# Earlier layernorm statistics, a later copy and a turned order of products in a pre-layernorm attention and feed-forward kernel

## The chip, the cores and the metric

The kernel runs on one core of a Trainium2 chip. The metric is the device time of one execution in microseconds (us). A core has five engines with a queue of instructions each, which run side by side and wait for each other by semaphores: TensorE (PE, matrix products and transposes; PEld is its loading of weights), VectorE (DVE), ScalarE (ACT), GpSimd (POOL) and SyncE (SP), which here only starts copies by DMA. PE writes to PSUM, a small memory of banks; all else lies in SBUF or in DRAM.

## The reference

Sixteen sequences of 256 positions with 256 channels, all in float32. Each goes through attention and then through a quantised linear layer, both behind a layernorm and both added to what came in:

```python
x = x + attention(layernorm(x), wq, wk, wv, wo)
x = x + ffn(layernorm(x), weight, bias)
```

The layernorm takes off the mean and divides by the root of the variance plus 1e-5, per position; it has no weights. Attention has 16 query heads and 4 key and value heads of 128 channels. A query sees the first 4 positions (the sink) and the last 32 up to itself (the window):

```python
mask = (k <= q) & ((k < 4) | (k >= q - 31))
scores = einsum(q, k) / sqrt(128);  attn = masked_softmax(scores);  out = (attn @ v) @ wo.T
```

The ffn scales each row of its input and of the weight to 127, rounds to int8, multiplies, scales back and adds the bias:

```python
x_q = round(x / (max|x| / 127));  y = (x_q @ w_q.T) * x_scale * w_scale + bias
```

## The kernel before

**Units and places.** The work is cut into 128 units: 16 sequences (n), times 4 groups of heads (g), times 2 halves of the queries (t). One loop (`for i in range(len(units) + 2)`) goes through them; its round i is called place i here, and place i modulo 8 "place 0 to 7 of a sequence". In every place the scores of one unit are computed (L556, into `pss`), DVE scales and masks them (L567) and takes the row maxima (L569), ACT does the exponentials (L594), and DVE takes the sums against a floor (L601), their reciprocals (L602) and the product (L613). DVE then transposes the weights by blocks of 32 (L578), and SP brings them through DRAM into the layout that the next product needs: the store `zd` (L580), and, from the next place on, the load `ad` (L584). Two places after its scores the unit's weights meet the values (L619, `po`); ACT copies the result (L631, `oT`). In the first three and the last units there is no way through DRAM: PE transposes (L561) and ACT copies (L564, `ad`).

**The other work** is hung on places by tables (`at(place, function, list)`). Each queue runs in the order in which the instructions are written; no scheduler changes it. In a place the order is: scores; work listed as `begin`; output products of older units (`shares`); exponentials; `combine` of the queries asked for in the place before; values and weights product (`po`); a chunk of keys or values if the place has one (even places); normalisation; the next queries; POOL's `combine` of the chunk; DVE's `combine` of a finished output (in place 3); and last the list `small`.

**Seven products instead of eight.** The products of queries, keys, values and output, cut into 2 x 2 blocks of 128, are done with seven block products, as in Strassen's method. Sums of blocks are prepared by POOL (L257 to L266: `xs` of the input, `wq_sums` and the like of the weights, `os` of the attention's output). The seven products lie in two PSUM banks: 1, 2, 6 and 7 in the first, 4, 5 and 3 in the second. `products` yields them in an order that is an argument: 1, 2, 6, 7, 4, 5, 3 unless another is given (the queries), or `SMALL_FIRST`, that is 4, 5, 3, 1, 2, 6, 7 (keys and values). `combine` makes the result of the seven with five additions (L304 to L308): the first two read the first bank, the last three the second. DVE does it for the queries (`qt`) and the output (`pc`), straight from PSUM; POOL does it for keys and values (`ktmp`, `vt`), from copies that ACT makes of the two banks (`both_banks`, L325: second bank first). Queries use the two banks of the pool `ps_q`; a chunk of keys or values takes its second bank from `ps_q` and its first from `ps_m`, which has two banks and is also used for `po`. The output's seven products are summed over the groups of heads in the pool `ps_y`, which has one pair of banks: the next sequence's first output products (place 4, L674) can start when `combine` has read the last ones.

**The first layernorm of sequence n** is spread over the places from 8n - 14 on: `load_x` (L94) at 8n - 16, statistics (`statistics`, L183 and L185 on DVE, L187 and L188 on POOL) at 8n - 14, that is place 2 of sequence n - 2, the two normalisations (L193) two and four places after the statistics, and then the transposition by blocks (L387, through DRAM with L392 and L401) and the channel sums (L263 to L266). For sequences 1 and 2 the places are given by hand.

**The second layernorm and the ffn of sequence n** are six steps (`ffn_steps`) in places 4, 5, 6 of sequence n + 1 and 0, 1, 2 of sequence n + 2: statistics, normalising (with the bias on POOL, L729), scale (L710, L711), quantising (L715 and L717 on DVE, L720 and L721 on POOL), a transposing copy by SP (L724, `hT`), and the linear layer (L735 on PE, L740 on DVE, L741 on POOL, and the store L742).

**The tail.** The last sequence's output ends in two halves, which go through `last_steps` one after the other: `stats`, `quantise`, `turn`, `linear` (L758 to L794). The first half's `stats` and `quantise` are written at the end of place 127, its `turn` at the end of place 128.

Of the kernel before, what the change touches and what calls it, by code (L numbers as in the profile page):

```python
# [34 lines left out]
def kernel(  # L35
# [12 lines left out]
    pe, dve, act, pool, sp = nc.tensor, nc.vector, nc.scalar, nc.gpsimd, nc.sync  # L48
# [42 lines left out]
    def load_x(n):  # L91
        if n < B:
            xts[n] = xp.tile([P, NT, DM], FP, tag="x", name=f"x_{n}")
            sp.dma_start(xts[n], x_v[n])  # L94
# [4 lines left out]
    wv_sb = const.tile([P, NC, G * D], FP, name="wv_sb")  # L99
# [147 lines left out]
    def region(p, i):  # L247
        return p[REGION[i][0]][:, REGION[i][1]]
# [16 lines left out]
        pool.tensor_sub(t[2], b22, b12)  # L265
        pool.tensor_sub(t[3], b21, t[1])  # L266

    def products(p, factors, order=(1, 2, 6, 7, 4, 5, 3)):

        a, sa, b, sb = factors  # L270
        pairs = {
            1: (a[0][0], b[0][0]), 2: (a[0][1], b[1][0]), 6: (sa[1], sb[1]), 7: (sa[2], sb[2]),
            4: (a[1][1], sb[3]), 5: (sa[0], sb[0]), 3: (sa[3], b[1][1]),
        }
        for i in order:
            yield region(p, i), *pairs[i]
# [4 lines left out]
    SMALL_FIRST = (4, 5, 3, 1, 2, 6, 7)  # L281
# [5 lines left out]
    def banks_of_chunk(name):  # L287
        p = [ps_m.tile([P, NBLK, P], FP, tag="m", name=f"{name}_0"), q_bank(0, f"{name}_1")]
        turn_of[0] ^= 1
        return p  # L290
# [48 lines left out]
    wv_sums = const.tile([P, 4, 2, D], FP, name="wv_sums")  # L339
# [6 lines left out]
    def factors(n, w, sums, pair):  # L346

        a = [[w[:, c, (2 * pair + e) * D : (2 * pair + e + 1) * D] for c in range(NC)] for e in range(2)]
        return (
            a, [sums[:, i, pair % 2] for i in range(4)],  # L350
            xn_blocks(n), [xn_sums[n][:, i] for i in range(4)],
        )

    def xn_blocks(n):
        return [[xnT[n][:, c, j * P : (j + 1) * P] for j in range(NT)] for c in range(NC)]

    def norm_steps(n):
        def stats():
            mvs[n] = statistics(xts[n], range(NT), f"a{n}")

        def norm(t):
            if t == 0:
                xns[n] = p1.tile([P, NT, DM], FP, tag="xn", name=f"xn_{n}")
            standardise(xns[n], xts[n], mvs[n], [t])

        return [stats, lambda: norm(0), lambda: norm(1)]

    def channels(n):

        xn_sums[n] = p2.tile([P, 4, P], FP, tag="xs4", name=f"xs4_{n}")  # L370
        b = xn_blocks(n)
        right_sums([xn_sums[n][:, i] for i in range(4)], *b[0], *b[1])

    def turned(n):
        xnT[n] = p2.tile([P, NC, T], FP, tag="xnT", name=f"xnT_{n}")
        pt = ps_m.tile([P, NC, T], FP, tag="m", name=f"xt_{n}")
        for c in range(NC):
            for j in range(NT):
                pe.transpose(pt[:, c, j * P : (j + 1) * P], xns[n][:, j, c * P : (c + 1) * P], ident)
        dve.tensor_copy(xnT[n], pt)  # L380
        channels(n)
# [56 lines left out]
    def values_buffer(n, pair):  # L438
        vw[n, pair] = vws[pair]

    def values_to(n, pair, v, tiles=range(NT)):


        w, fresh = vw[n, pair], n == 0
        b0, b1 = tiles[0] * NBLK, (tiles[-1] + 1) * NBLK
        sp.dma_start(w[1:NKP:NCH, b0:b1], v[b0:b1].rearrange("b k d -> k b d"))
        c1 = min(b1 + 1, SB)
        sp.dma_start(w[0:NKP:NCH, b0 + 1 : c1], v[b0 : c1 - 1].rearrange("b k d -> k b d"))
        if b0 == 0:
            rows = QB if fresh else SINK  # L450
            sp.dma_start(w[2 : NCH * (rows - 1) + 3 : NCH], v[0, 0:rows].unsqueeze(1).to_broadcast([rows, SB, 2 * D]))
            if fresh:
                sp.dma_start(w[0:NKP:NCH, 0], v[0])
# [45 lines left out]

    def values(n, pair):  # L500
        p = banks_of_chunk(f"pv_{n}_{pair}")
        for to, left, right in products(p, factors(n, wv_sb, wv_sums, pair), SMALL_FIRST):
            pe.matmul(to, right, left, start=True, stop=True)  # L503
        v = p2.tile([P, 3, 2, D], FP, tag="vt", name=f"vt_{n}_{pair}")

        def rest():
            vd = dram.tile([T, 2 * D], FP, tag="vd", name=f"vd_{n}_{pair}")
            sp.dma_start(vd.rearrange("(j p) d -> p j d", p=P), v[:, 0:2].rearrange("p j e d -> p j (e d)"))
            values_buffer(n, pair)
            return lambda: values_to(n, pair, vd.rearrange("(b k) d -> b k d", k=QB))  # L510

        return Products(p, f"v_{n}_{pair}", (v[:, 0:3:2, 0], v[:, 2, 1], v[:, 1, 0], v[:, 0:2, 1])), rest
# [233 lines left out]
    def last_steps(j):  # L746

        n, tag = B - 1, f"last_{j}"  # L750
        py = pys[n][j][:, 0:2].rearrange("p i d -> p (i d)")
        d = p1.tile([P, 2, 3, D], FP, tag="ktmp", name=f"d_{tag}")[:, 0, 0:2].rearrange("p i d -> p (i d)")
        x2 = p1.tile([P, 6, D], FP, tag="pc", name=f"x2_{tag}")[:, 0:2].rearrange("p i d -> p (i d)")
        y = p1.tile([P, NT, DM], FP, tag="xn", name=f"y_{tag}")[:, 0]
        mv = p2.tile([P, nc.vector.BN_AGGR_DIM], FP, tag="mv2", name=f"mv_{tag}")
        top, by, xs, least = (p2.tile([P, 1], FP, tag=k, name=f"{k}_{tag}") for k in ("top", "by", "xs1", "least"))
        hT = p2.tile([P, NC, P], BF, tag="hT1", name=f"hT_{tag}")

        def stats():
            st = p2.tile([P, nc.vector.BN_STATS_DIM], FP, tag="st2", name=f"st_{tag}")  # L760
            dve.bn_stats(st, py)
            dve.bn_aggr(mv, st)

            pool.tensor_scalar(least, mv[:, 1:2], LN_EPS, 1e-24, ALU.add, ALU.mult)
            pool.tensor_tensor(least, least, root, ALU.pow)
            pool.tensor_scalar(mv[:, 1:2], mv[:, 1:2], LN_EPS, None, ALU.add)
            pool.tensor_tensor(mv[:, 1:2], mv[:, 1:2], half[:, 0:1], ALU.pow)
            dve.tensor_scalar(d, py, mv[:, 0:1], None, ALU.subtract)
            dve.tensor_reduce(top, d, AX.X, ALU.max, apply_absolute_value=True)
            act.copy(x2, py)  # L770

        def quantise():
            dve.tensor_scalar(top, top, 1.0 / 127.0, least, ALU.mult, ALU.max)
            dve.reciprocal(by, top)
            pool.tensor_mul(xs, top, mv[:, 1:2])
            for c in range(NC):
                k = d[:, c * P : (c + 1) * P]
                dve.tensor_scalar(k, k, by, MAGIC, ALU.mult, ALU.add)
                dve.tensor_scalar(k, k, MAGIC + 127.0, MAGIC - 128.0, ALU.min, ALU.max)

        def turn():
            for c in range(NC):
                pt = (ps_s, ps_t)[c].tile([P, P], FP, tag="st"[c], name=f"ht_{tag}_{c}")
                pe.transpose(pt, d[:, c * P : (c + 1) * P], ident)
                dve.tensor_scalar(hT[:, c], pt, MAGIC, None, ALU.subtract)
            dve.tensor_add(x2, x2, bias_bc)

        def linear():
            pa = ps_m.tile([P, DM], FP, tag="m", name=f"pa_{tag}")
            for c in range(NC):  # L790
                pe.matmul(pa, hT[:, c], wqfT[:, c, :], start=(c == 0), stop=(c == NC - 1))
            dve.scalar_tensor_tensor(y, pa, xs, wsc_bc, ALU.mult, ALU.mult)
            dve.tensor_add(y, y, x2)
            sp.dma_start(out_v[n, :, j], y)  # L794

        return [stats, quantise, turn, linear]


# [20 lines left out]
    def at(slot, f, what=small):  # L819
        what.setdefault(slot, []).append(f)  # L820
# [14 lines left out]
            at(n * PER + slot, (n, h), asked)  # L835
    for n in range(1, B):
        first = n * PER - 14
        places = (0, 1, 1, 2) if n == 1 else (4, 5, 6, 7) if n == 2 else (first, first + 2, first + 4, first + 5)
        for k, slot in enumerate(places[:3]):
            at(slot, lambda n=n, k=k: norm_steps(n)[k]())  # L840
        if n == 1:
            at(places[3], lambda n=n: turned(n))
        else:
            def turn(n=n, slot=places[3]):
                for k, f in enumerate(turned_by_blocks(n)):
                    at(slot + 1 + k, f, begin)
                at(slot + 2, lambda: channels(n))

            at(places[3], turn)
            at(max(first - 2, 0), lambda n=n: load_x(n))  # L850
    for i, (n, g, t) in enumerate(units):
        if n == 0:
            at(i + 2 + lag(i), lambda u=(n, g, t): projected(*u), shares)
# [157 lines left out]
```

## Time and profile before

| what | value |
|---|---|
| time, median of 3 runs | 780.27 us (780.01 to 780.97) |
| time of the profiled execution | 780.31 us |
| its span, first to last instruction | 778.5 us |
| mean granted TensorE clock | 0.998 |
| busy: PE, DVE, POOL, ACT | 758.6, 624.7, 512.7, 399.4 us |
| copies by DMA | 97.45 MB, mean 125 GB/s |

A profiled row of the timeline gives the start in us from the span's start, the duration in us, the engine, the source line, the operation, what it writes and reads (buffer numbers left out), how many instructions are merged into the row, and in brackets the idle time before it with what ended it. A row of waits gives the engine and line that waited, the engine and line that it waited for, the total in us, how often, and the longest. Busy time is an average over stages; what counts for the end is which wait ends last at a place. Spans on POOL are rough.

### The profile page before, as it was taken

Reading aid. Unit: us, or ns where it says so; the run is one execution under the profiler, and the core shown is the slowest. Engines: PE = TensorE matmul, PEld = TensorE weight load, DVE = VectorE, ACT = ScalarE, POOL = GpSimd, SP = SyncE. Lnnn points to the kernel's source line nnn. Section 1 sums busy time; section 2 is a strip of 40 time slices with the busy share of each in tenths; the row PEclk is TensorE's granted clock in tenths of the full one; section 3 lists DMA queues with packets and bytes.
Section 4 is the critical chain, followed back from the end, with each engine's and each line's share of the span. In section 5 each row is a group of like instructions: output and inputs, shape, how many; then the busy total and the mean of one; then the engine's idle time right before and its main releaser. Section 6 shows DMA issues by size and latency. Waiting matters only on the chain.

```text
span 778.5 us, 18824 instructions
## 1 busy us (share of the span) xinstructions
PE 758.6 (97%) x6483; PEld 744.0 (96%) x6483; DVE 624.7 (80%) x1775; ACT 399.4 (51%) x1561; POOL 512.7 (66%) x812
## 2 busy tenths in 40 slices
PE   9999999999999999999999999999999999999995
PEld 7989999999999999999999999999999999999994
DVE  2578978888788887888889788888888879887765
ACT  3555545555455455554555455554554554555551
POOL 4666977676665856757676675866658577576622
PEclk9999999999999999999999999999999999999999
DMA  7625354343534435344254543435344353443311
GB/s 241 208 86 139 112 143 133 104 122 122 153 114 137 124 94 162 117 139 137 86 137 125 148 128 106 131 111 160 117 134 122 98 154 117 130 138 101 95 44 35
DMA packets 150679, 97.45 MB, mean 125 GB/s; under 512 B 44984, under 2 KB 148792, under 8 KB 150584
## 3 DMA queue, kind: packets, MB, share of 16 engines
q1 hardware_dynamic: 150584, 96.24, 42.1%
q8 instruction: 52, 0.85, 0.4%
q14 instruction: 43, 0.35, 0.2%
HBM read 54.39 MB, written 39.85 MB: 121 GB/s over the span
## 4 chain that ended last, share of the span: by engine, by line
PE 86%; DVE 11%; issue 2%; ACT 0%; POOL 0%; DVEq 0%; POOLq 0%; ACTq 0%
PE pq L523 21%; PE py L674 21%; PE po L619 13%; PE pss L556 11%; PE pk L493 6%; PE pv L503 6%; PE py L658 3%; DVE scores L613 2%; PE pq L534 2%; DVE y L740 1%; DVE sm L601 1%; PE pa L735 1%; DVE nmax L569 1%; DVE scores L567 1%; DVE qt L306 1%
## 5 line engine op out<-in xcount | busy, mean ns | idle before, releaser
L594 ACT ACTIVATE scores<-scores,nmax 128x68 f32<-128x68 f32 x512 | 173.5, 340 | 259.5 <-DVE nmax L569 257.0
L619 PE MATMUL po<-ad,vw 96*128 96x128 f32 x1024 | 135.4, 275 | 0.8 <-ACT ad L564 0.8
L556 PE MATMUL pss<-kt,qt 128*128 128x68 f32 x1024 | 130.2, 268 | 0.0
L619 PEld LDWEIGHTS po<-ad,vw 96*128 96x128 f32 x1024 | 125.5, 192 | 2.1 <-ACT ad L564 1.5
L556 PEld LDWEIGHTS pss<-kt,qt 128*128 128x128 f32 x1024 | 126.1, 192 | 0.7 <-issue 0.5
L567 DVE SCALAR_TENSOR_TENSOR scores<-pss,masks 128x272 f32<-128x272 f32 x128 | 56.2, 439 | 83.9 <-PE pss L556 82.6
L523 PE MATMUL pq<-xs,wq_sums 128*128 128x128 f32 x714 | 118.6, 275 | 0.0
L523 PEld LDWEIGHTS pq<-xs,wq_sums 128*128 128x128 f32 x714 | 98.8, 192 | 0.0
L594 ACT ACTIVATION_READ_ACCUMULATOR scores<-scores,nmax 128x1 f32 x512 | 95.7, 187 | 0.0
L674 PE MATMUL py<-wo_sums,os 128*128 128x128 f32 x672 | 87.0, 279 | 0.0
L631 ACT COPY oT<-po 128x512 f32<-128x512 f32 x129 | 75.4, 585 | 22.2 <-PE po L619 22.2
L304 POOL TENSOR_TENSOR ktmp<-b_k 128x256 f32<-128x256 f32 x30 | 25.6, 853 | 90.1 <-ACT b_k L325 90.1
L674 PEld LDWEIGHTS py<-wo_sums,os 128*128 128x128 f32 x672 | 79.5, 192 | 0.0
L578 DVE STREAM_TRANSPOSE z<-scores 128x384 f32<-128x384 f32 x120 | 69.4, 578 | 4.1
L523 PE MATMUL pq<-xnT,wq_sb 128*128 128x128 f32 x476 | 72.6, 275 | 0.0
L257 POOL TENSOR_TENSOR os<-oT 128x256 f32<-128x256 f32 x56 | 41.0, 732 | 45.9 <-ACT oT L631 45.9
L674 PE MATMUL py<-wo_sb,oT 128*128 128x128 f32 x448 | 62.2, 282 | 8.5 <-DVE pc L305 8.5
L613 DVE TENSOR_TENSOR scores<-scores,sm 128x272 f32<-128x272 f32 x120 | 61.5, 513 | 4.1
L674 PEld LDWEIGHTS py<-wo_sb,oT 128*128 128x128 f32 x448 | 54.5, 192 | 9.9 <-issue 9.9
L523 PEld LDWEIGHTS pq<-xnT,wq_sb 128*128 128x128 f32 x476 | 62.7, 192 | 0.0
L569 DVE TENSOR_REDUCE nmax<-scores 128x4 f32<-128x272 f32 x128 | 55.8, 436 | 4.4
L304 POOL TENSOR_TENSOR vt<-b_v 128x256 f32<-128x256 f32 x30 | 21.9, 730 | 51.3 <-ACT b_v L325 51.3
(186 smaller groups left out, 1729.0 us busy)
## 6 DMA issues: line engine op xcount, KB each, us to landing
zd<-z SPq DMA_DIRECT2D x120, 192.0 KB
ad<-zd SPq DMA_DIRECT2D x120, 192.0 KB
vd<-vt SPq DMA_DIRECT2D x30, 256.0 KB
vw<-vd SPq DMA_DIRECT2D x30, 256.0 KB
vw<-vd SPq DMA_DIRECT2D x30, 224.0 KB
x<-in_x_dram SPq DMA_DIRECT2D x15, 256.0 KB
out_dram<-y SPq DMA_DIRECT2D x15, 256.0 KB
zxd<-zx SPq DMA_DIRECT2D x56, 64.0 KB
```

The costliest lines, as they stand in the source:

```text
L304: eng.tensor_add(c11_u, like(p[0][:, 0:2], c11_u), two(p1, c11_u))
L493: pe.matmul(to, left, right, start=True, stop=True)
L523: pe.matmul(to, left, right, start=True, stop=True)
L556: pe.matmul(pss[:, k, :], qt[n, g][:, t, k].rearrange("p h i -> p (h i)"), kt[n, g][:, t * NBLK + k, :], start=True, stop=True,)
L567: dve.scalar_tensor_tensor(s[:, :, 0:NK], pss, SCALE, masks[:, t], ALU.mult, ALU.add)
L569: dve.tensor_reduce(nmax, s[:, :, 0:NK], AX.X, ALU.max, negate=True)
L578: dve.transpose(z, s.rearrange("p k (c i) -> p c k i", c=NCH))
L594: act.activation(s[:, k, 0:NK], s[:, k, 0:NK], AF.Exp, bias=nmax[:, k : k + 1], scale=1.0, accum_out=sm[:, k : k + 1],)
L613: dve.tensor_mul(s, s, sm.unsqueeze(2).to_broadcast([P, NBLK, NK]))
L619: pe.matmul(po[:, k], vw[n, g // 2][:, t * NBLK + k, g % 2 * D : (g % 2 + 1) * D], ad[:, :, k], start=True, stop=True,)
L631: act.copy(o[:, t, hs].rearrange("p h (k i) -> p k h i", i=QB), po[:, :, hs])
L674: pe.matmul(region(py, i), left[:, e], right[:, e], start=(g == 0 and e == 0 and i in (1, 4)), stop=(g == G - 1 and e == 1 and i in (7, 3)),)
```

## The change

Three edits.

1. The first layernorm's statistics of sequences 3 to 15 are done two places earlier, at 8n - 16 (place 0 of sequence n - 2); the load of x is issued two places earlier too, at 8n - 18 (place 6 of sequence n - 3). Normalisations and the rest stay.
2. In the tail, ACT's copy of the first half's output (`x2`) is written in `turn` instead of `stats`, and so stands in ACT's queue behind the copy of the last transposed weights (`ad`) and the two copies `oT`. For the second half it stays.
3. The first values of sequence 1 (pair 0, place 6 of sequence 0) take their seven products in the order 1, 2, 6, 7, 4, 5, 3 instead of 4, 5, 3, 1, 2, 6, 7.

```diff
-    def products(p, factors, order=(1, 2, 6, 7, 4, 5, 3)):
+    LARGE_FIRST = (1, 2, 6, 7, 4, 5, 3)
+
+    def products(p, factors, order=LARGE_FIRST):
...
     def values(n, pair):
         p = banks_of_chunk(f"pv_{n}_{pair}")
-        for to, left, right in products(p, factors(n, wv_sb, wv_sums, pair), SMALL_FIRST):
+
+        order = LARGE_FIRST if (n, pair) == (1, 0) else SMALL_FIRST
+        for to, left, right in products(p, factors(n, wv_sb, wv_sums, pair), order):
             pe.matmul(to, right, left, start=True, stop=True)
...
             dve.tensor_reduce(top, d, AX.X, ALU.max, apply_absolute_value=True)
-            act.copy(x2, py)
+            if j:
+                act.copy(x2, py)
...
         def turn():
+            if not j:
+                act.copy(x2, py)
             for c in range(NC):
...
         first = n * PER - 14
-        places = (0, 1, 1, 2) if n == 1 else (4, 5, 6, 7) if n == 2 else (first, first + 2, first + 4, first + 5)
+        places = (0, 1, 1, 2) if n == 1 else (4, 5, 6, 7) if n == 2 else (first - 2, first + 2, first + 4, first + 5)
...
-            at(max(first - 2, 0), lambda n=n: load_x(n))
+            at(max(first - 4, 0), lambda n=n: load_x(n))
```

## The prediction

> **What bounds the kernel now.** First the page's top, for who is busy; then what TensorE (PE) waited for; then the instructions in order of time at the place of the largest wait.
>
> ```profile
> span 778.5 us, 18824 instructions
> PE 758.6 (97%) x6483; PEld 744.0 (96%) x6483; DVE 624.7 (80%) x1775; ACT 399.4 (51%) x1561; POOL 512.7 (66%) x812
> ```
> PE is the bound: an edit away from PE pays only where PE waits today. Its waits (total, times, longest) are few:
>
> ```profile
> PE py L674 <- DVE pc L305: 8.5, 12, 0.7
> PE ht_last L784 <- DVE d_last L779: 3.1, 2, 2.9
> PE pv L503 <- DVE qt L305: 1.2, 1, 1.2
> PE po L619 <- ACT ad L564: 0.8, 1, 0.8
> ```
> The first row is one wait in each of sequences 2 to 13: the next sequence's first output products (place 4 of 8) stand behind VectorE's (DVE) reading of the old ones in `combine`, at the end of place 3. Below is why DVE is late there, in the sequence around 361 us, and beside it sequence 14, around 692 us, the only one with this `combine` in which place 2 carries no first-layernorm statistics (no sequence 16 exists).
>
> ```profile
> 360.94 0.72 POOL L188 TENSOR_TENSOR mv_a<-mv_a,half 128x2 f32<-128x2 f32 x1
> 361.63 1.27 POOL L741 TENSOR_TENSOR y<-y,x 128x512 f32<-128x512 f32 x1
> 363.10 0.73 POOL L257 TENSOR_TENSOR os<-oT 128x256 f32<-128x256 f32 x1 [0.20 <-ACT oT L631]
> ...
> 690.77 1.27 POOL L741 TENSOR_TENSOR y<-y,x 128x512 f32<-128x512 f32 x1
> ```
> ```profile
> 362.19 0.72 DVE L601 TENSOR_TENSOR sm<-sm,floor 128x4 f32<-128x4 f32 x1
> 363.16 0.96 DVE L613 TENSOR_TENSOR scores<-scores,sm 128x272 f32<-128x272 f32 x1
> 365.08 0.29 DVE L305 TENSOR_TENSOR pc<-py,pc 128x128 f32<-128x128 f32 x1
> ...
> 692.47 0.16 DVE L601 TENSOR_TENSOR sm<-sm,floor 128x4 f32<-128x4 f32 x1
> 692.88 0.44 DVE L613 TENSOR_TENSOR scores<-scores,sm 128x272 f32<-128x272 f32 x1
> 694.28 0.29 DVE L305 TENSOR_TENSOR pc<-py,pc 128x128 f32<-128x128 f32 x1
> ```
> ```profile
> 365.51 1.13 PE L674 MATMUL py<-wo_sb,oT 128*128 128x128 f32 x8 [0.71 <-DVE pc L305]
> ...
> 694.92 1.11 PE L674 MATMUL py<-wo_sb,oT 128*128 128x128 f32 x8
> ```
> L601 is stretched to 0.72 us and ends at 362.91, when GpSimd's (POOL) L741 ends (362.90); L613 then falls into L257 and takes 0.96. In sequence 14 POOL has no L187/L188 to do before L741, which ends at 692.04, before L601 starts; both run at 0.16 and 0.44, and PE does not wait. So the delay comes not from DVE's own load (its statistics end at 358.12 and it then idles 0.74 us for PE) but from POOL being 1.00 us late (L187 starts 360.63, L741 361.63).
>
> **The change, part by part.**
>
> *Statistics of sequences 3 to 15, from place 2 to place 0.* Moved each time: two bn_stats and two bn_aggr on DVE (357.19 to 358.12, 0.93), L187 and L188 on POOL (1.00), and one 256 KB load of x, issued in place 6 instead of place 0 (issue 0.42 to 1.20 on SyncE's (SP) queue).
>
> What goes: 12 waits. Sequence 14 shows the whole price: from place 4's scores to place 5's takes 694.08 to 700.44 = 6.36 us there, 363.80 to 371.24 = 7.44 in the sequence shown. 1.08 each, 12 x 1.08 = 12.96. It is more than the row's 0.71 because PE also drags behind DVE after the wait (the keys' first products at 368.04, 0.15 after L305 of the queries). What is late next: at 697.24 PE starts the keys 0.15 after DVE's 697.09, so it is just DVE-bound there even then; 6.36 includes that.
>
> What it costs in place 0:
> ```profile
> 347.88 0.44 DVE L567 SCALAR_TENSOR_TENSOR scores<-pss,masks 128x272 f32<-128x272 f32 x1 [1.34 <-PE pss L556]
> ...
> 357.52 0.73 POOL L304 TENSOR_TENSOR vt<-b_v 128x256 f32<-128x256 f32 x1 [1.16 <-ACT b_v L325]
> ```
> DVE idles 1.34 us before place 1's scores; 0.93 fits, 0.41 is left. L717 (0.88, two instructions) slides beside POOL's adds of the keys, where such a pair costs up to 0.3 (L304 took 0.99 beside L717 instead of 0.73): about 0.1 is left. If that is gone, scores of place 1 come late by tenths, and the next cover is 0.88 of DVE idle at 353.01, while PE's first reuse of a query bank (350.41) stands 0.97 after DVE freed it (349.44). Cost 0, bounds 0 and, if DVE ran over by a whole 0.3 with no cover, 12 x 0.3 = 3.6.
>
> POOL: L720 and L721 (quantise), the four L257 to L260 and the four channel sums run 1.00 later, 356.36 becoming 357.36, and the 1.16 of idle before place 2's adds takes it: these wait for ScalarE's (ACT) copy until 357.52 anyway. Behind L720/L721 queue: the transposing copy L724 on SP (352.53, to about 353.1), behind it the weights' copy `ad` of place 1 (354.13, used 361.34) and, through the data, PE's L735 at 358.22. L724 was issued as late as 5.01 us before L735 (164.47 against 169.48) without a wait; 353.1 is 5.1 before. The sums `os` end at 355.6, used about 359.5; the channel sums are used three places later. Cost 0.
>
> SP: in place 6 the load now stands between `vd` (337.79) and the copy `ad` (338.32), which goes to about 338.8 and shares the engines with 256 KB more. Its reader is PE's po at 342.81, 4.0 us later. The nearest row is place 4's: `ad` issued at 363.41 right behind a 256 KB store, read at 367.02, 3.6 us, no wait. `vd`'s reader in place 7 and the later zd stay in order. In place 0 the load is gone from in front of `ad` (348.52). Cost 0; bounds 0 and 13 x 0.5 = 6.5, if it landed 0.5 us past its reader. x is read two places after its issue, as before.
>
> *Order of products in the second sequence's first values.* Place 6 of sequence 0:
> ```profile
> 49.31 0.46 PE L503 MATMUL pv<-wv_sb,xs 128*128 128x128 f32 x2 [1.20 <-DVE qt L305]
> ```
> PE was free at about 47.9 and waited for the query bank, freed at 49.16. With products 1, 2, 6, 7 first, four (0.89, as 50.05 to 50.95) go at once into the other bank, free since ACT's copy at 45.4. Then 49.31 again for 4, 5, 3 (0.67), to 49.98; the queries behind need the second query bank, which DVE's L308 frees at 50.14, so they start at 50.29 instead of 50.95. Their own 4, 5, 3 at 51.2 need ACT's first copy of the values, from about 50.2 to 50.7: no wait. Gain 0.66; PE has no wait again before 129 us, and DVE (free at 52.84) meets the earlier scores at 52.89. Bounds: 0, if that copy is late, and 0.89.
>
> *The tail's copy.* ACT's `x2` copy (764.85) held the last `ad` copy, and PE waited 0.82 for it. Now `ad` can go at 763.3, and po at 764.94 instead of 765.76. But PE's next instruction is the transpose L784, which waits for DVE's L779 (767.00), which hangs on POOL's L765 (765.97) behind L741 (763.77 to 765.03). None of these moves: PE just waits longer there. The copy, behind the two oT copies (about 766.75), ends near 767.1, and its reader L786 runs at 768.15. Gain 0; bounds 0.82 (the whole wait) and a loss of 0.37 (the copy's length).
>
> Sum: 780.31 (the profiled execution; span 778.5) - 12.96 - 0.66 - 0 = 766.69. The median of the runs, 780.27, is 0.04 lower; so 766.7.
>
> **The rivals.**
>
> *POOL carries its lateness into place 2.* L741 would end 0.43 before L601, and the shift leaves another 0.09 (357.43 against 357.52). A carry beyond 0.52 costs what exceeds it: 0.8 gives 12 x 0.28 = 3.4, 770.1; at 1.0 L613 meets L257 again and all 1.08 are lost, 779.6. For it: L601 and L613 of places 1 and 2 get new neighbours. Against: in those places POOL's L265 and L266 kept 0.46 and 0.45 beside them, and it was L601 that stretched (0.46).
> The Trainium skill (SBUF — State Buffer, Who interferes with whom) says that a Vector instruction with two SBUF inputs and a GpSimd instruction reading SBUF exclude each other, and the later one waits for the whole of the earlier. By that rule it is open who loses, and if POOL lost at every meeting (0.16 + 0.44 in each of two places, 1.2) the gain would be gone, 779.6; the stretched L601 and L613 agree with the rule, with POOL first.
>
> *Slower: `ad` of place 6 lands late.* Each us beyond 342.81 stalls PE in place 0 thirteen times. It decides from 13.62 / 13 = 1.05 us late, landing 5.1 us after issue; at 1.5 us late, 766.7 + 19.5 = 786.2. For: two 256 KB transfers just ahead. Against: before, `vd` and `ad` together moved between 338.6 and 340.5; 256 KB more ends near 341.6.
>
> *It does not do what sequence 14 shows*, the wait having another cause: only the 0.66 stays, 779.6. For: sequence 14 also lacks the later norm steps. Against: those come after place 4's wait.
>
> *More than forecast*: the tail's 0.82 and 12 x 0.11 (7.44 against the usual 6.25 is 1.19): 764.5.
>
> **How the numbers follow.** Forecast 0.67 (own range 765.5 to 768.5), more 0.06, partial carry 0.12, no effect or full carry 0.06, late `ad` or another new wait worth over 13 us 0.09. The range 764.8 to 772.0 takes in the forecast, most of "more", the partial carry and the small unknown costs, and leaves out about 0.18. A measurement tells 0.2% (1.6 us) from no change. Faster 0.85, same 0.06, slower 0.09.
>
> **What will show it.** Right: no row of PE waiting for pc L305, L601 at 0.16 and L613 at 0.44 in place 3, L741 directly behind L308 of the values, the sequence's period 46.1 instead of 47.18; pv's wait about 0.5 in its middle; the wait at po gone and that at L784 longer by as much. Wrong: rows of PE waiting for `ad` or for hT, DVE scores not waiting for PE in place 1, or L741 ending after L601's start.

## The result, and the profile after

The changed kernel takes 768.52 us (median of 4 runs, 767.44 to 769.72), the kernel before 780.46 beside it (780.01 to 780.97): ratio 0.9847, 95% interval 0.983 to 0.9864. Forecast was 766.7. The profiled execution took 767.44 (span 765.7), 12.87 less than before's. In the changed kernel line numbers are two higher from L267 on and four higher from L507 on (L305 is L307, L601 is L605, L613 is L617, L674 is L678, L717 is L721, L741 is L745), five to seven higher in the tail (L779 is L784, L784 is L791).

The top of the page and the waits of PE (total in us, times, longest), after:

```profile
span 765.7 us, 18824 instructions
PE 754.4 (99%) x6483; PEld 742.4 (97%) x6483; DVE 621.8 (81%) x1775; ACT 399.2 (52%) x1561; POOL 511.7 (67%) x812
```
```profile
PE ht_last L791 <- DVE d_last L784: 4.3, 3, 2.9
PE warm L891 <- POOL half L132: 1.3, 1, 1.3
PE po L623 <- DMA ad<-zd: 0.4, 1, 0.4
PE pv L507 <- DVE qt L307: 0.3, 1, 0.3
```
The row of 12 waits for `pc` is gone, and so is the tail's wait for ACT's `ad`; the tail's wait at the transpose has grown from 3.1 to 4.3. The wait for the first values fell from 1.2 to 0.3. One row is new: a wait for the weights' copy `ad`.

Rows from places 1 to 3 of the sequence around 355 us in the timeline of after, POOL and then DVE. Place 1 begins at 341.03 on DVE, place 3 has the rows from 356.72 on; rows between are left out:

```profile
344.07 0.71 POOL L188 TENSOR_TENSOR mv_a<-mv_a,half 128x2 f32<-128x2 f32 x1
344.87 0.61 POOL L724 TENSOR_SCALAR h<-h 128x512 f32<-128x512 f32 x1
345.56 1.50 POOL L725 TENSOR_SCALAR h<-h 128x512 bf16<-128x512 f32 x1
352.05 0.73 POOL L306 TENSOR_TENSOR vt<-b_v 128x256 f32<-128x256 f32 x1
355.03 1.28 POOL L745 TENSOR_TENSOR y<-y,x 128x512 f32<-128x512 f32 x1
357.62 0.73 POOL L257 TENSOR_TENSOR os<-oT 128x256 f32<-128x256 f32 x1 [1.31 <-ACT oT L635]
```
```profile
341.03 1.23 DVE L721 SCALAR_TENSOR_TENSOR h<-h,xr,magic 128x256 f32<-128x256 f32 x2
342.40 0.44 DVE L571 SCALAR_TENSOR_TENSOR scores<-pss,masks 128x272 f32<-128x272 f32 x1
344.89 0.60 DVE L605 TENSOR_TENSOR sm<-sm,floor 128x4 f32<-128x4 f32 x1
345.74 0.73 DVE L617 TENSOR_TENSOR scores<-scores,sm 128x272 f32<-128x272 f32 x1
356.72 0.16 DVE L605 TENSOR_TENSOR sm<-sm,floor 128x4 f32<-128x4 f32 x1
357.12 0.44 DVE L617 TENSOR_TENSOR scores<-scores,sm 128x272 f32<-128x272 f32 x1
358.52 0.29 DVE L307 TENSOR_TENSOR pc<-py,pc 128x128 f32<-128x128 f32 x1
```
and PE at the start of place 4:
```profile
359.16 1.11 PE L678 MATMUL py<-wo_sb,oT 128*128 128x128 f32 x8
```
L745 ends at 356.31, 0.41 before L605 starts; L605 and L617 have their short lengths 0.16 and 0.44, `pc` is read by 358.81, and PE starts its products at 359.16 without a wait. The collisions have moved to place 1, where POOL is now later by L187 and L188: L605 takes 0.60 beside L724 and L617 0.73 beside L725, and PE waits for neither. L721 there was stretched from 0.88 to 1.23, and 0.14 us of DVE's idle time was left before the scores.

**Where the 12.87 us came from.** By the starts of L735 (L739 after), from one sequence to the next: before 47.18 or 47.19 in twelve sequences and 46.10 in the last; after 46.11 in all but one, which has 46.62. That is 12 x 1.075 = 12.90, less 0.51. The first L735 starts at 122.30 before and at 121.70 after: 0.60. So the last one starts 12.90 + 0.60 - 0.51 = 12.99 earlier (762.18 against 749.19). From there to the end it is 16.5 instead of 16.3. That is not accounted for further; in the ten profiles whose tail is that of the kernel before or of the change, this stretch is 16.3 to 16.7.

The 0.51 is the new row, in place 4 of one sequence, behind the store of `y`:
```profile
176.14 1.16 PE L623 MATMUL po<-ad,vw 96*128 96x128 f32 x8 [0.36 <-DMA ad<-zd]
```

### The profile page after: what moved, and what is told of

Read it like the earlier page. It is cut to its first block, busy times and chain, and to the rows that moved or that the text cites. A ratio compares the mean times of both kernels' runs of the same rounds, so it can differ in the third digit from the quotient of the medians.

```text
span 765.7 us, 18824 instructions
## 1 busy us (share of the span) xinstructions
PE 754.4 (99%) x6483; PEld 742.4 (97%) x6483; DVE 621.8 (81%) x1775; ACT 399.2 (52%) x1561; POOL 511.7 (67%) x812
## 4 chain that ended last, share of the span: by engine, by line
PE 96%; DVE 2%; DMA 1%; ACT 0%; POOL 0%; issue 0%; DVEq 0%; POOLq 0%; ACTq 0%
PE pq L527 24%; PE py L678 23%; PE po L623 15%; PE pss L560 14%; PE pk L495 6%; PE pv L507 6%; PE py L662 3%; PE pq L538 2%; PE pa L739 1%; DMA ad<-zd 1%; PE warm L891 1%; PE pv L470 0%; PE pk L461 0%; PE ptd L565 0%; ACT scores L598 0%
## 5 line engine op out<-in xcount | busy, mean ns | idle before, releaser
L678 PE MATMUL py<-wo_sums,os 128*128 128x128 f32 x672 | 87.0, 279 | 0.0
L678 PEld LDWEIGHTS py<-wo_sums,os 128*128 128x128 f32 x672 | 79.5, 192 | 0.0
L306 POOL TENSOR_TENSOR ktmp<-b_k 128x256 f32<-128x256 f32 x30 | 22.4, 746 | 84.3 <-ACT b_k L327 84.3
L617 DVE TENSOR_TENSOR scores<-scores,sm 128x272 f32<-128x272 f32 x120 | 60.3, 503 | 4.1
L678 PE MATMUL py<-wo_sb,oT 128*128 128x128 f32 x448 | 62.0, 281 | 0.0
L678 PEld LDWEIGHTS py<-wo_sb,oT 128*128 128x128 f32 x448 | 54.5, 192 | 0.0
L308 DVE TENSOR_TENSOR qt<-pq,qt 128x256 f32<-128x256 f32 x119 | 50.5, 424 | 4.0
```

The lines of the kernel that those rows point to most:

```text
L308: eng.tensor_add(c21_c22, like(p[1][:, 0:2], c21_c22), v.unsqueeze(1).to_broadcast(c21_c22.shape))
L617: dve.tensor_mul(s, s, sm.unsqueeze(2).to_broadcast([P, NBLK, NK]))
L678: pe.matmul(region(py, i), left[:, e], right[:, e], start=(g == 0 and e == 0 and i in (1, 4)), stop=(g == G - 1 and e == 1 and i in (7, 3)),)
```

## The experiments

Each set ran on one chip with the kernel before beside it. The first four take the change apart.

**GpSimd's two small instructions alone.** The theory of the prediction is that POOL being 1.00 late makes L601 and L613 long. `statistics` of sequence n stays in place 2 with its load in place 0; only its add and power on POOL go to the end of place 3:

```diff
+        if later is None:
+            roots()
+        else:
+            later.append(roots)
...
+        if n > 2:
+            at(first + 1, lambda: roots_late.pop(0)())
```


> The kernel before, with one thing moved: the two GpSimd instructions of the first layernorm's statistics (add epsilon, power) go from place 2 to the end of place 3; VectorE's four stay in place 2 and the load of x stays in place 0. Theory (GpSimd's lateness is the cause): the wait for pc L305 goes, the sequences' period falls from 47.18 to 46.1, the time to 780.4 - 13.0 = 767.4. Rival (VectorE's own statistics make it late): nothing or little moves, 780.4.

Measured 767.42 us (767.14 to 767.76, 4 runs), ratio 0.9833 (0.9818 to 0.9848). Waits of PE:
```profile
PE ht_last L793 <- DVE d_last L788: 3.1, 2, 2.9
PE warm L895 <- POOL half L132: 1.3, 1, 1.3
PE pv L512 <- DVE qt L312: 1.2, 1, 1.2
PE po L628 <- ACT ad L573: 0.8, 1, 0.8
```
No wait for `pc`, none for `ad`, and every sequence takes 46.1. The other waits are those of before, but for one of 0.3 at the start of the program (`xt`). So 12.7 us come from 1 us of GpSimd, moved by one place; DVE's four statistics instructions could have stayed where they were.

**Everything but those two.** DVE's statistics in place 0 and the load in place 6, as changed; L187 and L188 stay in place 2:

```diff
-        places = (0, 1, 1, 2) if n == 1 else (4, 5, 6, 7) if n == 2 else (first, first + 2, first + 4, first + 5)
+        places = (0, 1, 1, 2) if n == 1 else (4, 5, 6, 7) if n == 2 else (first - 2, first + 2, first + 4, first + 5)
...
+        if n > 2:
+            at(first, lambda: roots_late.pop(0)())
...
-            at(max(first - 2, 0), lambda n=n: load_x(n))
+            at(max(first - 4, 0), lambda n=n: load_x(n))
```


> The other half alone: VectorE's four statistics go to place 0 and the load of x to place 6, as in the change, but GpSimd's two instructions stay in place 2, ahead of the addition of L741. Theory (GpSimd's lateness is the cause): L601 is stretched as before, the wait for pc stays, the period stays 47.18, 780.4. Rival (VectorE's statistics): 767 to 768. If the earlier load costs by itself, it shows here as a time above 780.4 and as rows of TensorE waiting for ad.

Measured 781.66 us (780.61 to 782.46, 10 runs), ratio 1.0017 (1.0008 to 1.0026): slower.
```profile
PE py L683 <- DVE pc L312: 8.6, 12, 0.7
PE po L628 <- DMA ad<-zd: 1.1, 3, 0.6
```
The `pc` row has not changed at all, so DVE's own load in place 2 was no part of that wait. The new row is `ad`: two sequences take 47.79 and 48.01 instead of 47.18, that is 0.61 + 0.83 = 1.44, and the third wait comes ahead of the first L735, which starts at 122.58 instead of 122.30. All three are in place 0, behind the load. This execution took 782.35, which is 2.04 more than the profiled one of before: the three waits make 1.44 + 0.28 of that, and 0.3 lies behind the last L744, where the same tail varies by as much. No cost of DVE's statistics in place 0 is seen there. By the medians about 0.25 is left for it: 1.51 is lost here, and 1.26 with the load alone (below), on another chip.

**The order of products alone.**

```diff
-        for to, left, right in products(p, factors(n, wv_sb, wv_sums, pair), SMALL_FIRST):
+        for to, left, right in products(p, factors(n, wv_sb, wv_sums, pair), (1, 2, 6, 7, 4, 5, 3) if (n, pair) == (1, 0) else SMALL_FIRST):
```


> Only the order of products in the second sequence's first values. Theory: 0.6 less, 779.8, the whole timeline from the first linear layer on 0.6 earlier. Rival (the next wait takes it back): same time, and the linear layer's first product at 122.3 as before.

Measured 779.47 us (779.07 to 780.42, 11 runs) against 780.15, ratio 0.9989 (0.9981 to 0.9998): 0.68 less. The same place in this run, where PE had waited 1.20 before any of the seven:
```profile
48.44 0.61 PE L503 MATMUL pv<-wv_sb,xnT 128*128 128x128 f32 x4
48.89 0.61 PE L503 MATMUL pv<-wv_sums,xs 128*128 128x128 f32 x4
49.80 0.46 PE L503 MATMUL pv<-wv_sb,xs 128*128 128x128 f32 x2 [0.30 <-DVE qt L305]
...
50.78 0.46 PE L523 MATMUL pq<-xnT,wq_sb 128*128 128x128 f32 x2
```
Four products run while the query bank is still taken; 0.30 of wait is left. From the `po` ahead of this place (47.50) to these queries it is 3.28; before it was 3.95 (47.00 to 50.95).

The profiled execution was the slowest of the eleven, 780.42. Its first L735 starts at 122.22, only 0.08 earlier than before, which is what the rival of the expectation named. The rest was lost ahead of this place, where that `po` starts 0.50 later; PE waited at the very start of the program, which it does not do in the profile of before:
```profile
PE xt L420 <- DVE xn L193: 1.2, 2, 0.7
```
In the five profiles without the new order the first product of the linear layer starts between 122.11 and 122.58, in the eight others with it between 120.98 and 121.73.

**The tail's copy alone.**

```diff
-            act.copy(x2, py)
+            if j:
+                act.copy(x2, py)
...
         def turn():
+            if not j:
+                act.copy(x2, py)
```


> Only the tail's copy of x2 behind the copy of the last weights. Theory: the wait of 0.82 at po goes and the wait at the transpose of the tail grows by as much; time 780.4, nothing within 0.2. Rival: the 0.82 is gained, 779.6.

Measured 780.2 us (779.81 to 780.74, 11 runs), ratio 0.9998 (0.9989 to 1.0006). The `ad` row of the tail is gone, and PE waits longer at the next instruction, where two waits of 3.1 in all have become three of 4.3:
```profile
PE ht_last L787 <- DVE d_last L780: 4.3, 3, 2.9
```
```profile
764.68 1.06 PE L619 MATMUL po<-ad,vw 96*128 96x128 f32 x8
766.96 0.33 PE L787 MATMUL ht_last<-ident,d_last 128*128 128x128 f32 x1 [1.23 <-DVE d_last L780]
```

The next two ask where the 1.8 us between the forecast and the median went; the suspect is the load of x, which now stands ahead of `ad` on SP's queue in place 6.

**The load alone.**

```diff
-            at(max(first - 2, 0), lambda n=n: load_x(n))
+            at(max(first - 4, 0), lambda n=n: load_x(n))
```


> The kernel before with only the load of x two places earlier, in place 6 between the store vd and the load ad; the statistics stay in place 2. Theory (the moved load makes the ad read in place 0 late in some sequences): about 1.5 more, 781.7, rows of TensorE waiting for ad some 32 after the linear layer's first product, longest 0.5 to 0.8. Rival (the loss came from VectorE's statistics in place 0): 780.2 and no such rows.

Measured 781.30 us (781.03 to 781.92, 11 runs) against 780.04, ratio 1.0017 (1.0008 to 1.0026): 1.26 slower. The waits, then the queue of SP and PE's `po` in one of the two sequences that wait:
```profile
PE py L674 <- DVE pc L305: 8.5, 12, 0.7
PE po L619 <- DMA ad<-zd: 0.6, 2, 0.4
```
```profile
385.25 0.37 SPq L508 DMA_DIRECT2D vd<-vt  x1
385.67 0.46 SPq L94 DMA_DIRECT2D x<-in_x_dram  x1
386.23 0.44 SPq L584 DMA_DIRECT2D ad<-zd  x1
...
389.01 1.11 SPq L448 DMA_DIRECT2D vw<-vd  x1
```
```profile
390.88 1.16 PE L619 MATMUL po<-ad,vw 96*128 96x128 f32 x8 [0.44 <-DMA ad<-zd]
```
`ad` is issued behind two copies of 256 KB and read 390.88 - 386.23 = 4.65 after its issue; in a sequence without a wait the distance is 4.05. The two sequences take 47.63 and 47.89, 0.45 + 0.71 = 1.16 over the usual. A DMA issue behind it, `vw`, took 1.11 where it otherwise takes 0.60; what else was moving then stands under "Left open".

**The change with the load one place earlier still**, in place 5, where no `vd` goes out ahead of it:

```diff
-            at(max(first - 4, 0), lambda n=n: load_x(n))
+            at(max(first - 5, 0), lambda n=n: load_x(n))
```


> The changed kernel with the load of x yet one place earlier, in place 5, where it stands between zd and ad and no vd is near; the ad behind it is read in place 7. Theory (it is vd, the load and ad in a row that is too much): no row of TensorE waiting for ad in place 0, 766.8 with little spread. Rival (statistics in place 0, or a load anywhere earlier, cost the same): 768.5.

Measured 766.76 us (766.65 to 767.07, 4 runs), ratio 0.9831 (0.9817 to 0.9844), no row for `ad`, all sequences 46.11. That is the sum of the prediction, to 0.1.

Because these differences are small, both were run again in one set on another chip:

> The kernel with the load in place 5 once more, beside the two above and the changed kernel on one chip: 766.8, without rows of TensorE waiting for ad.

> The changed kernel once more, unchanged, for another profiled execution: 768.5, and one to four rows of TensorE waiting for ad in place 0 or 4 that together make what it takes above 766.8. Rival (its excess is elsewhere): 768.5 without such rows.

With the load in place 5: 767.53 us (766.77 to 768.44, 4 runs). The change itself: 768.34 (767.39 to 770.02, 5 runs). The order of the two is the same, but the difference is 0.8 here and the runs overlap, so its size is not settled by the times. The profile of the change in this set says more:

```profile
245.15 1.16 PE L623 MATMUL po<-ad,vw 96*128 96x128 f32 x8 [0.27 <-DMA ad<-zd]
383.95 1.16 PE L623 MATMUL po<-ad,vw 96*128 96x128 f32 x8 [0.22 <-DMA ad<-zd]
```
Both are in place 0, behind the load, in the same two sequences as with the load alone. Four sequences exceed 46.11: by 0.53 and 0.48 (these two) and by 0.29 and 0.24 (place 4, behind the store of `y`, with no row of a wait for `ad`), 1.54 together; 766.8 + 1.54 = 768.3, and this execution took 768.40. With the load in place 5 the profile of this set has one sequence over 46.11, by 0.13.

**Can the tail gain as well?** The moved copy gave nothing because the transpose hangs on POOL's L765 behind L741. So four kernels hold back the last add of sequence 14 (L741) and its store. The first two have the order of products and the roots in place 3 (as in the first experiment), and write the add after the first half's `stats` and `quantise`; one copies `x2` where the kernel before does, the other where the change does.

```diff
-            pool.tensor_add(y, y, xt)
-            sp.dma_start(out_v[n], y)
+            def close_out():
+                pool.tensor_add(y, y, xt)
+                sp.dma_start(out_v[n], y)
+
+            if n == B - 2:
+                closing.append(close_out)
+            else:
+                close_out()
```


> The kernel before with GpSimd's two instructions of the statistics in place 3 and the new order of products (766.8 by the runs so far), and in the tail GpSimd's last addition of L741 and its store behind the first half's stats and quantise; the copy of x2 stays in stats, ahead of the copy of the last weights. Theory (the transposes of the tail hang on that addition): the square roots on GpSimd come 0.74 earlier, but po, late by its 0.82, then holds TensorE: 0.3 less, 766.5. Rival (the tail hangs on something else): 766.8.

> The same, and the copy of x2 in turn, as in the change. Theory (with the addition out of the way the copy's place pays): 0.74 less than without both, 766.1, 0.4 under the kernel with the copy in stats. Rival (the copy is worth nothing in any case): equal to the kernel with the copy in stats.

Measured 766.98 us (766.74 to 769.2, 5 runs) and 767.21 (766.74 to 767.71, 4 runs): no gain over 766.76. The chain moved up, and at its end the add collided with it, here with the copy later, DVE and POOL:
```profile
752.21 0.23 DVE L797 TENSOR_SCALAR d_last<-d_last 128x128 f32<-128x128 f32 x1
752.67 1.17 DVE L797 TENSOR_SCALAR d_last<-d_last 128x128 f32<-128x128 f32 x1
```
```profile
752.44 1.31 POOL L753 TENSOR_TENSOR y<-y,x 128x512 f32<-128x512 f32 x1
```
```profile
753.98 0.30 PE L804 MATMUL ht_last<-ident,d_last 128*128 128x128 f32 x1 [1.16 <-DVE d_last L797]
```
The second clamp takes 1.17 instead of 0.23 and ends at 753.84, just after the add (753.75), and PE waits for it.

So the last pair adds a copy of one element on POOL, which reads what the clamps write, and the add queues behind it. These two have the change and the load in place 5:

```diff
+            if not j:
+                mark = p2.tile([P, 1], FP, tag="mark", name="mark")
+                pool.tensor_copy(mark, d[:, DM - 1 : DM])
```


> The kernel with the load in place 5 (766.8), and in the tail GpSimd's last addition and its store held, by a one-element copy that reads what VectorE's last clamp of the first half writes, until that clamp is done; the copy of x2 in turn. Theory (the addition ahead delays the transposes, the addition beside the clamps stretched one of them from 0.23 to 1.17): first transpose 0.74 earlier, no clamp above 0.3, the tail 0.7 shorter, 766.0. Rival (it comes back in another collision behind the clamps): 766.8 or more.

> The same with the copy of x2 in stats, ahead of the copy of the last weights. Theory (once GpSimd's addition is out of the way the place of the copy pays): the wait at po is back and the tail 0.4 longer than with the copy in turn, 766.4. Rival (the place of the copy is worth nothing in any case): 766.0.

Measured 767.87 us (767.04 to 768.84, 4 runs) and 767.14 (766.39 to 767.75, 4 runs), beside 767.53 for the same kernel without it in this set. From the last L739 to the last pair of transposes it is 10.55 in the change, 9.97 here, and 10.36 with the copy first; so the tail is 0.6 shorter, and once the add is out of the way the copy's place is worth 0.39. To DVE's last instruction 0.4 of it is left (12.72 against 13.14), and the times don't show even that. The add now meets DVE's L804 behind the clamps, which takes 1.06 instead of 0.41, as the rival of the expectation had it. In the first of the two the profile shows why:
```profile
PE po L623 <- DMA ad<-zd: 1.2, 2, 0.9
```
Two sequences, 46.62 and 47.15, lose 0.51 + 1.04 = 1.55 to `ad` in place 4. That is more than the tail gives.

## Why the prediction was right, and where it was not

- *Twelve waits of 1.08, because POOL is 1.00 late*: right in cause and size. 12 x 1.075 = 12.90 against 12.96; GpSimd's two instructions alone give 12.7, and DVE's statistics alone leave the `pc` row as it was. That also settles the rival "it does not do what sequence 14 shows".
- *DVE in place 0, cost 0*: right, and as narrow as said. About 0.1 of idle time was forecast to be left, 0.14 was. L717's stretch was 0.35 (1.23 against 0.88) where up to 0.3 was allowed.
- *POOL, cost 0*: right. POOL's adds of the values start at 352.05, 0.08 after ACT's second copy of them has ended, as before (357.52 after 357.45); the idle time ahead of them is down from 1.16 to 0.12, and no lateness is carried to L745. The Trainium skill (SBUF — State Buffer, Who interferes with whom) has DVE and GpSimd exclude each other on such operands, by the order in which they come. The trace agrees for L605, which took 0.60 and ended 0.01 after L724. For L617 it does not: L617 was stretched to 0.73, but ended 0.59 before L725, which had started ahead of it (spans on POOL are rough). In place 1 it was again DVE that lost; in place 2 both lost a little (L605 0.35, L617 0.57, POOL's L265 0.66 instead of 0.46). So the rival "POOL loses at every meeting" did not come about.
- *SP: the load ahead of `ad` in place 6, cost 0*: this step failed. It measured 1.26 alone; in the two profiles of the change it is 0 and 1.0. The distance from issue to read was right (4.05, said 4.0). What was wrong is the reading of the nearest row: place 4's 3.6 us stand behind one copy of 256 KB, and from one sequence, while here two stand ahead; and "ends near 341.6" took the copies' speed of one stretch for that of all thirteen. In two sequences `ad` came later than its reader could bear, by 0.18 and 0.44 with the load alone. The rival "late `ad`" was the right mechanism, in two sequences of thirteen instead of all.
- *Not in the sum at all*: `ad` of place 4. It cost 0.51 in the profiled execution, 0.53 in the later one, 1.55 in a variant, and no profile of a kernel that keeps the `pc` wait has it. That PE, no longer held up ahead of this place, has too little room there for a slow copy fits this, but is argued and not shown: GpSimd's two instructions alone take the same wait away, and that profile has no late `ad`. The load in place 6 is no condition for it: the variant that holds back the add and copies later has the load in place 0, waits 0.15 for `ad` in place 4 of one sequence, and takes 46.42 there. The prediction looked for what is late next on DVE and not at SP's copies.
- *Order of products, 0.66*: right, 0.60 in the profile and 0.68 in the times. The remaining wait is 0.30, not about 0.5.
- *Tail's copy, 0*: right, and for the reason given: the wait moved to the transpose, whole.
- *The "more" rival* fell: neither the tail's 0.82 nor 12 x 0.11 came.

The sum to 766.7 is what the kernel does with the load out of the way on one chip (766.76); on another it took 767.53, 0.8 more. The profiled execution differs from 766.69 by the 0.51 of place 4, the tail's 0.2 and the roundings above. The median is 1.1 above that execution, and the later profile puts such an excess down to `ad`.

Left open in part: why `ad` is late in the same few sequences of otherwise different kernels, and why in one execution in place 0 and in another in place 4. The records of the DMA queues show what goes with it. Besides the copies (queue q1), every profile has 52 packets of 16 KB on a queue that the page calls `instruction` (q8), each of 0.9 to 1.9 us. From 376 to 383 in the second profile of the change, around the `ad` that is issued at 379.53 and waited for at 383.95 (queue: packets, MB, share):

```profile
q1 hardware_dynamic: 1175, 1.03, 44.7%
q8 instruction: 1, 0.02, 0.9%
```
All 11 waits for `ad` behind a DMA, in six of the 14 profiles, have such a packet, which started 1.24 to 2.43 after the issue of that `ad`. In the nine kernels or repeats without the `pc` row, ten sequences exceed 46.2 by place 4; each has a packet that started 0.05 to 1.94 after the issue there. One at 0.03 cost 0.02; where it started 3.0 or more after, or none did, nothing is lost in place 4. In the five profiles that keep the `pc` row no packet fell into that stretch, so they do not tell whether PE would have had room. In place 0 behind the load a packet is not enough: five that started 2.13 to 2.46 after the issue cost nothing. No run moved these packets, so it is an inference from these coincidences, and not shown by an experiment, that they make `ad` late. Why a packet falls at 1.46 in one execution and at 3.11 in another, in the same sequence, stays open.

Loading x in place 5 has the lowest median of all (766.76), below each of the change's first runs, but not clearly ahead of the change where both ran on one chip; no kernel here is reliably under 766.7.

## What to carry to other kernels

When an engine waits for a slow instruction, look at whom that instruction collides with: here 1 us of tiny GpSimd work set the time of DVE's instructions, and moving only that would have given the gain without touching the loads. A step that is moved takes its DMA with it; price that load by the worst of the copies behind it, not by one row, since one late copy in a few sequences is enough to pay, and look at what else the DMA queues carry in those sequences. And when a wait on the bound engine is removed, list what had been hiding behind it, the copies too.

## What the runs showed of the hardware

- A 192 KB copy read 4.05 us after its issue, behind two 256 KB copies, was in time in most sequences and late in a few, with waits of 0.18 to 0.55. The late ones recur in the same sequences of different kernels.
- DMA issues on SP's queue are slow beside packets of the `instruction` queues (q8, 16 KB; q14, 8 KB). In the 14 profiles 143 issues took over 0.3 us more than the median of their line and shape (as 1.11 above), and all 143 ran beside such a packet; of the 6885 others 868 did.
- The loss in a sequence is larger than the wait in the row: 0.44 waited and 0.71 lost, 0.36 and 0.51. With `pc` it was 0.71 and 1.08.
- An instruction of DVE with a single SBUF input is stretched as well: the clamp over 128 x 128 took 1.17 instead of 0.23 beside a GpSimd add of 1.31. The Trainium skill (SBUF — State Buffer, Who interferes with whom) has this for scalar operations of DVE in modes that use two ports, where the later instruction waits for the whole of the earlier. The trace agrees in that the clamp ended 0.09 after the add; which mode it ran in no run shows.
